# Last sequence of a fused Hawk and RWKV layer: gate chunks paired across the two gate weights, recurrences placed under gate products

## The chip, the cores and the metric

The kernel runs on one core of one Trainium2 chip. The metric is device time in microseconds. Three runs of the kernel before the change gave 657.23, 657.51 and 657.99 us, a median of 657.51 us.

## The reference

The input x has 8 sequences of 1024 tokens with 256 features, all in float32. The layer normalizes x, feeds the result to two blocks, and adds both to x:

```python
xn = _layernorm(x)
# block 1 (Hawk), 384 channels
gate = xn @ Wg.T ; u = xn @ Wi.T
y  = causal_depthwise_conv(u, conv_w, 4 taps) + conv_b
ig = sigmoid(y @ lru_Wi.T + lru_bi)
rg = sigmoid(y @ lru_Wg.T + lru_bg)
alpha = exp(-8 * softplus(lam) * rg)
beta  = sqrt(1 - alpha**2 + 1e-6)
h[t]  = alpha[t] * h[t-1] + beta[t] * ig[t] * y[t]     # along the tokens
hawk  = (gelu(gate) * h) @ Wo.T
# block 2 (RWKV channel mix), 256 channels
r = sigmoid(mix_r(xn) @ W_r.T) ; k = mix_k(xn) @ W_k.T
ffn = r * (square(relu(k)) @ W_v.T)
out = x + hawk + ffn
```

The recurrence over h is the only step that runs along the tokens. The product with Wo for a group of tokens needs gelu(gate) * h of all 384 channels for those tokens.

## The kernel before

**Layout.** Channels lie on the 128 partitions, tokens along the free dimension. The 384 channels are three chunks of 128 (HC = 3), numbered m = 0, 1, 2. A sequence of 1024 tokens has two halves of 512, L and R (HALVES). Tiles that matter here: y (the convolved input), tr (first tanh of the rg gate, then alpha), ti (tanh of the ig gate, then the input of the recurrence), q (first 1 - alpha**2, then beta, then h) and g (gelu(gate), then gelu(gate) * h). A sigmoid is computed as a tanh of half the argument, so ti has to be turned into (1 + ti) * 0.5 * beta * y before the recurrence.

**Gate products.** Both gate weights stand side by side in one tile w_l: rows 0 to 2 are the three chunks of the rg gate (they go to tr), rows 3 to 5 those of the ig gate (to ti). A Group (L194) makes two rows for both token halves at once. It uses a scheme with seven products in place of eight for two of the three input chunks, and adds the third input chunk with four plain products: 11 matmuls of 128x512 in all. The scheme needs sums of weight blocks (weight_sums, L157, on GpSimd, once per kernel for each family) and sums of token blocks (y_sums, L422, on GpSimd). Its five steps are s1 (2 matmuls), s2 (3), s3 (3), s4 (2) and s5 (1). Between them ScalarE copies a partial product to another bank and one to SBUF (seed L219, five L224), and VectorE adds them (fork_c L233, fork_d L247). After steps 2 to 5 ScalarE takes out one half of one row each through tanh (l_out, L326 and L329): row A half L after s2, row A half R after s3, row B half L after s4, row B half R after s5. In the kernel before, a group pairs rows 2*pair and 2*pair + 1: group 0 makes tr of chunks 0 and 1, group 1 makes tr of chunk 2 and ti of chunk 0, group 2 makes ti of chunks 1 and 2.

**Output products.** outs(s, t) (L597) makes the Wo product for two tiles of 128 tokens: six matmuls of 128x256 (by_token, L461, three chunks for each tile), then add_hawk (L505) adds the bank to the residual on VectorE and SyncE stores it. values (L591) does the same for the W_v product. A float32 matmul of the program is two MATMUL instructions in the profile.

**Recurrence.** For each chunk: decay (L538, Exp on ScalarE), decay_square (L542, Square on ScalarE), decay_rest (L545, VectorE), beta (L548, Sqrt on ScalarE), the input of the recurrence on VectorE, recur (L565, a scan on VectorE), and gated_state (L570, VectorE), which multiplies g by h. In sequences 0 to 6 the tail of this chain runs under the first products of the following sequence (chain, L606). The last sequence has no following one. There, all of the chain stands in the branch at L788 to L828, and the only PE work that is kept back for it is outs(s - 1, ...), the output products of the sequence before; the last four outs(s, ...) depend on the chain itself.

**Order.** Nothing is chosen by a scheduler. Every step is put into a list with a time (at, L183; pe, L186, which advances a clock by the length of a PE step), the list is sorted by that time (L836), and the instructions are issued in that order. The times are only sort keys: they fix the order on each engine's queue, and each engine then runs its queue in order, waiting for the semaphores of what it needs. There are eight PSUM banks, taken from and given back to a free list in the same order.

The branch before the change keeps d = now() right after the third step of group 1, and hangs the chain on it:

```python
for m in range(HC):
    at(d + [-2, -1.9, 0.2][m], decay, m)
    at(d + [-1, -0.9, 1][m], decay_square, m)
    at(d + [0, 1.2, 3][m], decay_rest, m)
    at(d + 3.1 + m / 10, beta, m)
    at(d + 9.2 + m / 10, weighted_input, m)
```

Of the kernel before, what the change touches and what calls it, by code (L numbers as in the profile page):

```python
# [32 lines left out]
def kernel(  # L33
# [120 lines left out]
    def block(family, row, c):  # L154
        return families[family][:, c, row * P : (row + 1) * P]

    def weight_sums(family):  # L157

        pairs = families[family].rearrange("p c (n r m) -> p c r n m", r=2, m=P)
        s = sums[family]  # L160
        a11, a12, a21, a22 = (pairs[:, c, r, :, :] for r in range(2) for c in range(2))
        nc.gpsimd.tensor_tensor(s[:, 0], a21, a22, ALU.add)
        nc.gpsimd.tensor_tensor(s[:, 1], s[:, 0], a11, ALU.subtract)
        nc.gpsimd.tensor_tensor(s[:, 2], a11, a21, ALU.subtract)
        nc.gpsimd.tensor_tensor(s[:, 3], a12, s[:, 1], ALU.subtract)
# [28 lines left out]
    class Group:  # L194


        def __init__(self, name, family, pair, chunk, tsum, out, third=None):
            self.name, self.family, self.pair, self.chunk, self.tsum = name, family, pair, chunk, tsum
            self.out, self.third = out, third
            self.bank = {}  # L200

        def step(self, n):
# [3 lines left out]
            def A(r, c):  # L206
                return block(self.family, 2 * self.pair + r, c)

# [116 lines left out]

    def l_out(gi, r, h, src):  # L326
        m = (2 * gi + r) % HC
        dst, b = (tr, HC) if 2 * gi + r < HC else (ti, 0)
        nc.scalar.activation(  # L329
            dst[:, m, HALVES[h]], src, AF.Tanh, bias=half_b[:, b + m : b + m + 1], scale=0.5  # L330
        )

    def u_group(s, gi):
# [3 lines left out]
            "u",  # L337
            gi,
            lambda c, h: xnT[:, c, 1 + h * NT : 1 + (h + 1) * NT],
            xsum,  # L340
            lambda r, h, src: place(gi, r, h, src),
        )

    def l_group(s, gi):
        return Group(
            f"l{gi}_{s}",
            "l",
            gi,
            lambda c, h: y[:, c, HALVES[h]],
            ysum,  # L350
            lambda r, h, src: l_out(gi, r, h, src),
            third=lambda h: y[:, 2, HALVES[h]],
        )
# [106 lines left out]

    def by_token(w, lhs, t, chunks):  # L461

        b = take()
        for j in range(2):
            for c in range(chunks):
                nc.tensor.matmul(  # L466
                    banks[b][:, j * D : (j + 1) * D],
                    lhs[:, c, (t + j) * P : (t + j + 1) * P],
                    weights[w][:, c, :],
                    start=(j == 0 and c == 0),  # L470
                    stop=True,
                    skip_group_check=True,
                )
        return b
# [27 lines left out]
    def o_product(s, t):  # L502
        token_bank["o", s, t] = by_token("o", gs[s % 2], t, HC)

# [52 lines left out]

    def weighted_input(m):

        nc.vector.scalar_tensor_tensor(q[:, m, :], q[:, m, :], 0.5, y[:, m, :], ALU.mult, ALU.mult)  # L560

    def opened_input(m, p):
        nc.vector.scalar_tensor_tensor(ti[:, m, p], ti[:, m, p], 1.0, q[:, m, p], ALU.add, ALU.mult)  # L563

    def recur(m, p=slice(0, S)):  # L565
# [24 lines left out]

    def values(s, t):  # L591
        pe(f"v{t}_{s}", 2, v_product, s, t)
        at(now() + 0.1, value, t)
        if t % 4 == 2:
            at(now() + 0.6, add_value, s, t // 4)

# [34 lines left out]
    with tc.manual_schedule():  # L631
# [61 lines left out]
        for s in range(B):  # L693
# [94 lines left out]
            else:  # L788
                gates(s, 4)
                gates(s, 6)  # L790
                values(s, 0)
                values(s, 2)
                at(now() - 1, y_sums)
                ls[0].step(1)
                values(s, 4)
                ls[0].step(2)
                ls[1].step(1)
                values(s, 6)
                ls[0].step(3)
                ls[1].step(2)  # L800
                ls[0].step(4)
                ls[2].step(1)
                ls[0].step(5)
                ls[1].step(3)
                d = now()
                outs(s - 1, 0)
                ls[1].step(4)
                ls[1].step(5)
                ls[2].step(2)
                outs(s - 1, 2, add=d + 13.6)  # L810
                ls[2].step(3)
                outs(s - 1, 4, add=d + 18)
                ls[2].step(4)
                ls[2].step(5)
                outs(s - 1, 6, add=d + 21.8)
                for t in range(0, TT, 2):
                    outs(s, t, 2)
                L, R = HALVES
                for m in range(HC):
                    at(d + [-2, -1.9, 0.2][m], decay, m)  # L820
                    at(d + [-1, -0.9, 1][m], decay_square, m)
                    at(d + [0, 1.2, 3][m], decay_rest, m)
                    at(d + 3.1 + m / 10, beta, m)
                    at(d + 9.2 + m / 10, weighted_input, m)
                for m, p, t in ((0, L, 13.2), (0, R, 13.3), (1, L, 13.5), (2, L, 20.3), (1, R, 20.4), (2, R, 21.3)):
                    for n, f in enumerate((opened_input, recur)):
                        at(d + t + 0.01 * n, f, m, p)
                    at(d + t + 0.03, gated_state, s, m, p)  # L828

# [66 lines left out]
```

## Time and profile before

| What | Value |
|---|---|
| Median of three runs | 657.51 us (657.23 to 657.99) |
| The profiled execution's own time | 657.73 us |
| Its span, first to last instruction | 655.9 us |
| PE busy | 646.9 us, 99% of the span |
| VectorE busy | 470.7 us, 72% |
| ScalarE busy | 430.3 us, 66% |
| GpSimd busy | 113.0 us, 17% |
| Mean granted TensorE clock | 0.995 |

The profile is of one execution. In the prediction its lines are in microseconds from the start of the span. In a timeline, the columns are the start, the time from the start of the first to the end of the last instruction of the group, the engine, the line of the kernel, the operation, output<-input, the number of instructions, and in brackets the idle time of the engine before the group with the work that ended it. Matmuls overlap, so the duration of a group is a little longer than the distance to the start of the next. PEclk is the share of full TensorE speed that the chip granted.

### The profile page before, as it was taken

The page shows a single profiled execution, that of the slowest core. Times are in us where ns is not written, and L with a number is a line of the kernel's source. Part 1 is how long each engine was busy: PE and PEld are TensorE (multiplying, and loading weights), DVE is VectorE, ACT ScalarE, POOL GpSimd, SP SyncE. Part 2 cuts the span into 40 slices and gives each one's busy share as a digit, 9 for nine tenths or more (in the row PEclk, how much of TensorE's full clock was granted, in tenths as well). Part 3 has the DMA queues.
Part 4 walks back from the last instruction along what each step waited for, and adds up shares of the span by engine and source line. Part 5 has one row for each costly group of instructions (what it writes and reads, how often), then busy time and mean ns, then how long its engine had stood idle before and what let it go on. Part 6 is the DMA issues. An engine that isn't in the chain of part 4 may idle for free.

```text
span 655.9 us, 5889 instructions
## 1 busy us (share of the span) xinstructions
PE 646.9 (99%) x2048; PEld 377.2 (58%) x2048; DVE 470.7 (72%) x604; ACT 430.3 (66%) x615; POOL 113.0 (17%) x82
## 2 busy tenths in 40 slices
PE   9999999999999999999999999999999999999987
PEld 4465446854477544775448654586445864466556
DVE  4778869755896659947599475993669844798295
ACT  4786877368782788727885388845878358772840
POOL 3606100430004300123003220042000430022000
PEclk9999999999999999999999999999999999999998
DMA  9402100031001400014000140001200011000012
GB/s 319 130 1 73 56 0 1 32 112 50 0 1 48 145 0 1 1 48 145 0 0 1 62 132 0 0 1 49 80 0 1 23 42 64 0 1 0 0 49 80
DMA packets 27550, 28.71 MB, mean 44 GB/s; under 512 B 1152, under 2 KB 27008, under 8 KB 27520
## 3 DMA queue, kind: packets, MB, share of 16 engines
q1 hardware_dynamic: 27104, 27.92, 12.9%
q10 hardware_dynamic: 416, 0.41, 0.2%
q8 instruction: 16, 0.26, 0.2%
q14 instruction: 14, 0.11, 0.1%
HBM read 19.94 MB, written 8.39 MB: 43 GB/s over the span
## 4 chain that ended last, share of the span: by engine, by line
PE 93%; DVE 4%; ACT 2%; issue 0%; DVEq 0%
PE bank L175 62%; PE bank L466 28%; PE bank L394 2%; PE bank L656 1%; DVE q L568 1%; ACT tr L540 1%; DVE q L560 1%; ACT q L543 0%; DVE g L572 0%; DVE ti L563 0%; DVE y L529 0%; DVE xr L439 0%; DVE res L510 0%; DVE st L367 0%; ACT L549 0%; ACT L540 0%
## 5 line engine op out<-in xcount | busy, mean ns | idle before, releaser
L175 PE MATMUL bank<-y,w_l 128*128 128x512 f32 x288 | 137.8, 592 | 0.0
L529 DVE SCALAR_TENSOR_TENSOR y<-u,par,y 128x1024 f32<-128x1024 f32 x72 | 94.3, 1326 | 1.2
L466 PE MATMUL bank<-w_o,g 128*128 128x256 f32 x384 | 89.9, 388 | 3.2 <-DVE g L572 3.1
L175 PEld LDWEIGHTS bank<-y,w_l 128*128 128x128 f32 x288 | 54.6, 190 | 62.6 <-issue 60.5
L466 PEld LDWEIGHTS bank<-w_o,g 128*128 128x128 f32 x384 | 74.8, 195 | 21.5 <-issue 6.2
L169 POOL TENSOR_TENSOR ysum<-y 128x512 f32<-128x512 f32 x8 | 16.9, 2106 | 385.4 <-PE bank L466 341.3
L175 PE MATMUL bank<-ysum,sum_l 128*128 128x512 f32 x144 | 72.4, 592 | 0.0
L219 ACT COPY bank<-bank 128x512 f32<-128x512 f32 x47 | 27.0, 575 | 66.2 <-PE bank L175 65.1
L233 DVE TENSOR_TENSOR bank<-bank,five 128x512 f32<-128x512 f32 x47 | 32.8, 698 | 51.4 <-PE bank L175 37.8
L175 PE MATMUL bank<-xsum,sum_u 128*128 128x512 f32 x138 | 69.1, 592 | 0.0
L329 ACT ACTIVATE tr<-bank,half_b 128x512 f32<-128x512 f32 x48 | 32.8, 684 | 54.5 <-PE bank L175 54.5
L175 PE MATMUL bank<-xk,w_k 128*128 128x512 f32 x128 | 60.1, 592 | 0.0
L466 PE MATMUL bank<-w_r,xr 128*128 128x256 f32 x256 | 57.7, 379 | 0.0
L466 PEld LDWEIGHTS bank<-w_r,xr 128*128 128x128 f32 x256 | 48.6, 190 | 13.1 <-issue 7.0
L175 PE MATMUL bank<-xnT,w_u 128*128 128x512 f32 x108 | 54.1, 593 | 0.2 <-ACT xnT L413 0.2
L466 PE MATMUL bank<-w_v,ysum 128*128 128x256 f32 x224 | 49.5, 379 | 0.0
L510 DVE TENSOR_TENSOR res<-res,bank 128x512 f32<-128x512 f32 (+1 forms) x36 | 22.0, 624 | 35.9 <-PE bank L466 35.9
L466 PEld LDWEIGHTS bank<-w_v,ysum 128*128 128x128 f32 x224 | 42.6, 190 | 5.8
L175 PEld LDWEIGHTS bank<-xsum,sum_u 128*128 128x128 f32 x138 | 26.1, 189 | 33.1 <-issue 31.2
L175 PEld LDWEIGHTS bank<-ysum,sum_l 128*128 128x128 f32 x144 | 26.8, 190 | 30.2 <-issue 28.5
L247 DVE TENSOR_TENSOR bank<-bank,five 128x512 f32<-128x512 f32 x24 | 16.7, 696 | 37.6 <-PE bank L175 37.6
L329 ACT ACTIVATE ti<-bank,half_b 128x512 f32<-128x512 f32 x48 | 30.3, 681 | 19.4 <-PE bank L175 19.3
(101 smaller groups left out, 1014.9 us busy)
## 6 DMA issues: line engine op xcount, KB each, us to landing
res<-in_x_dram SPq DMA_DIRECT2D x8, 1024.0 KB, 5.6
x<-in_x_dram SPq DMA_DIRECT2D x7, 1024.0 KB, 5.6
out_dram<-res SPq DMA_DIRECT2D x28, 256.0 KB, 2.1
x<-in_x_dram SPq DMA_DIRECT2D x4, 256.0 KB, 4.4
out_dram<-res SPq DMA_DIRECT2D x8, 128.0 KB, 1.8
w_l<-in_lru_wg_dram SPq DMA_DIRECT2D x1, 576.0 KB, 5.9
w_l<-in_lru_wi_dram SPq DMA_DIRECT2D x1, 576.0 KB, 6.9
w_u<-in_w_i_dram ACTq DMA_DIRECT2D x1, 384.0 KB, 4.0
```

Source lines behind the costliest of these rows:

```text
L169: nc.gpsimd.tensor_tensor(dst[:, 0, :], b12, b11, ALU.subtract)
L175: nc.tensor.matmul(banks[b], lhsT, rhs, start=start, stop=True, skip_group_check=True)
L219: nc.scalar.copy(banks[bank["B"]], banks[bank["A"]])
L233: nc.vector.tensor_tensor(banks[bank["C"]], banks[bank["B"]], self.five, ALU.add)
L247: nc.vector.tensor_tensor(d, banks[bank["B"]], self.five, ALU.add)
L329: nc.scalar.activation(dst[:, m, HALVES[h]], src, AF.Tanh, bias=half_b[:, b + m : b + m + 1], scale=0.5)
L394: nc.tensor.matmul(banks[b][:, t * P : (t + 1) * P], xs[s % 2][:, 4 * h + t, c * P : (c + 1) * P], ident, is_transpose=True, start=(t == 0 ...
L466: nc.tensor.matmul(banks[b][:, j * D : (j + 1) * D], lhs[:, c, (t + j) * P : (t + j + 1) * P], weights[w][:, c, :], start=(j == 0 and c == 0),
L510: nc.vector.tensor_tensor(o, o, two_tiles(b)[:, j : j + n, :], ALU.add)
L529: nc.vector.scalar_tensor_tensor(y[:, m, :], u[:, m, k : k + S], column(COL_CONV_W + k * HC + m), y[:, m, :], ALU.mult, ALU.add,)
L540: nc.scalar.activation(tr[:, m, :], tr[:, m, :], AF.Exp, bias=r, scale=r)
L560: nc.vector.scalar_tensor_tensor(q[:, m, :], q[:, m, :], 0.5, y[:, m, :], ALU.mult, ALU.mult)
```

## The change

Only the last sequence and its helpers change.

- Group gets its two rows as an argument. In the last sequence rows_of pairs row pair with row pair + 3: group 0 makes tr and ti of chunk 0, group 1 those of chunk 1, group 2 those of chunk 2. weight_sums is called a second time, for w_l with this pairing.
- The order of the PE steps of the last sequence is changed. Three of the four output products of the sequence before, outs(s - 1, 2), (4) and (6), stand behind the last gate product; outs(s - 1, 0) stands between the second and third step of group 2. d now marks the end of group 0, e the end of group 2.
- Two steps of VectorE for each chunk and half (weighted_input for the chunk, opened_input for the half) are replaced by gated_input and scaled_input, the pair that the earlier sequences use. The chains of chunks 0 and 1 are put under the products of groups 1 and 2, the scan of chunk 1 as one of 1024 tokens. Chunk 2 still goes in halves.
- In the first output product of the last sequence, the six matmuls go chunk by chunk (abreast) rather than token tile by token tile.
- The additions of the values (add_value) of the first half and of the output products of the sequence before stand at other places of VectorE's queue.

The diff:

```diff
@@ -154,9 +154,14 @@
     def block(family, row, c):
         return families[family][:, c, row * P : (row + 1) * P]
 
-    def weight_sums(family):
-
-        pairs = families[family].rearrange("p c (n r m) -> p c r n m", r=2, m=P)
+
+    def rows_of(pair, apart):
+        return (pair, pair + HC) if apart else (2 * pair, 2 * pair + 1)
+
+    def weight_sums(family, apart=False):
+
+        order = "p c (r n m) -> p c r n m" if apart else "p c (n r m) -> p c r n m"
+        pairs = families[family].rearrange(order, r=2, m=P)
         s = sums[family]
         a11, a12, a21, a22 = (pairs[:, c, r, :, :] for r in range(2) for c in range(2))
         nc.gpsimd.tensor_tensor(s[:, 0], a21, a22, ALU.add)
@@ -194,7 +199,8 @@
     class Group:
 
 
-        def __init__(self, name, family, pair, chunk, tsum, out, third=None):
+        def __init__(self, name, family, pair, rows, chunk, tsum, out, third=None):
+            self.rows = rows
             self.name, self.family, self.pair, self.chunk, self.tsum = name, family, pair, chunk, tsum
             self.out, self.third = out, third
             self.bank = {}
@@ -204,7 +210,7 @@
             S = [sums[self.family][:, i, self.pair, :] for i in range(4)]
 
             def A(r, c):
-                return block(self.family, 2 * self.pair + r, c)
+                return block(self.family, self.rows[r], c)
 
             bank = self.bank
             extra = 1 if third else 0
@@ -323,9 +329,9 @@
 
         return place
 
-    def l_out(gi, r, h, src):
-        m = (2 * gi + r) % HC
-        dst, b = (tr, HC) if 2 * gi + r < HC else (ti, 0)
+    def l_out(row, h, src):
+        m = row % HC
+        dst, b = (tr, HC) if row < HC else (ti, 0)
         nc.scalar.activation(
             dst[:, m, HALVES[h]], src, AF.Tanh, bias=half_b[:, b + m : b + m + 1], scale=0.5
         )
@@ -336,19 +342,22 @@
             f"u{gi}_{s}",
             "u",
             gi,
+            rows_of(gi, False),
             lambda c, h: xnT[:, c, 1 + h * NT : 1 + (h + 1) * NT],
             xsum,
             lambda r, h, src: place(gi, r, h, src),
         )
 
     def l_group(s, gi):
+        rows = rows_of(gi, s == B - 1)
         return Group(
             f"l{gi}_{s}",
             "l",
             gi,
+            rows,
             lambda c, h: y[:, c, HALVES[h]],
             ysum,
-            lambda r, h, src: l_out(gi, r, h, src),
+            lambda r, h, src: l_out(rows[r], h, src),
             third=lambda h: y[:, 2, HALVES[h]],
         )
 
@@ -458,19 +467,21 @@
         ka = key_home(s)
         nc.scalar.activation(ka[:, :, HALVES[h]], ka[:, :, HALVES[h]], AF.Square)
 
-    def by_token(w, lhs, t, chunks):
+    def by_token(w, lhs, t, chunks, abreast=False):
 
         b = take()
-        for j in range(2):
-            for c in range(chunks):
-                nc.tensor.matmul(
-                    banks[b][:, j * D : (j + 1) * D],
-                    lhs[:, c, (t + j) * P : (t + j + 1) * P],
-                    weights[w][:, c, :],
-                    start=(j == 0 and c == 0),
-                    stop=True,
-                    skip_group_check=True,
-                )
+        order = [(j, c) for j in range(2) for c in range(chunks)]
+        if abreast:
+            order.sort(key=lambda jc: jc[1])
+        for j, c in order:
+            nc.tensor.matmul(
+                banks[b][:, j * D : (j + 1) * D],
+                lhs[:, c, (t + j) * P : (t + j + 1) * P],
+                weights[w][:, c, :],
+                start=(j == 0 and c == 0),
+                stop=True,
+                skip_group_check=True,
+            )
         return b
 
     token_bank = {}
@@ -500,7 +511,7 @@
         nc.vector.scalar_tensor_tensor(o, tf[:, 4 * h : 4 * h + 4, :], 0.5, o, ALU.mult, ALU.add)
 
     def o_product(s, t):
-        token_bank["o", s, t] = by_token("o", gs[s % 2], t, HC)
+        token_bank["o", s, t] = by_token("o", gs[s % 2], t, HC, s == B - 1 and t == 0)
 
     def add_hawk(s, t, pieces=1):
         b = token_bank.pop(("o", s, t))
@@ -555,13 +566,6 @@
     def scaled_input(m, p=slice(0, S)):
         nc.vector.scalar_tensor_tensor(ti[:, m, p], ti[:, m, p], 0.5, q[:, m, p], ALU.mult, ALU.mult)
 
-    def weighted_input(m):
-
-        nc.vector.scalar_tensor_tensor(q[:, m, :], q[:, m, :], 0.5, y[:, m, :], ALU.mult, ALU.mult)
-
-    def opened_input(m, p):
-        nc.vector.scalar_tensor_tensor(ti[:, m, p], ti[:, m, p], 1.0, q[:, m, p], ALU.add, ALU.mult)
-
     def recur(m, p=slice(0, S)):
 
         before = 0.0 if p.start == 0 else q[:, m, p.start - 1 : p.start]
@@ -588,11 +592,11 @@
         pe(f"r{t}_{s}", 2, r_product, t)
         at(now() + 0.1, r_tanh, t)
 
-    def values(s, t):
+    def values(s, t, add=0.6):
         pe(f"v{t}_{s}", 2, v_product, s, t)
         at(now() + 0.1, value, t)
         if t % 4 == 2:
-            at(now() + 0.6, add_value, s, t // 4)
+            at(now() + add, add_value, s, t // 4)
 
     def outs(s, t, pieces=1, add=0):
         pe(f"o{t}_{s}", 3, o_product, s, t)
@@ -789,43 +793,64 @@
                 gates(s, 4)
                 gates(s, 6)
                 values(s, 0)
-                values(s, 2)
+                values(s, 2, 8)
+                at(b + 8, weight_sums, "l", True)
                 at(now() - 1, y_sums)
                 ls[0].step(1)
                 values(s, 4)
                 ls[0].step(2)
                 ls[1].step(1)
+                ls[0].step(3)
                 values(s, 6)
-                ls[0].step(3)
+                ls[0].step(4)
                 ls[1].step(2)
-                ls[0].step(4)
+                ls[0].step(5)
+                d = now()
                 ls[2].step(1)
-                ls[0].step(5)
                 ls[1].step(3)
-                d = now()
-                outs(s - 1, 0)
                 ls[1].step(4)
                 ls[1].step(5)
                 ls[2].step(2)
-                outs(s - 1, 2, add=d + 13.6)
+                outs(s - 1, 0, add=d + 15.2)
                 ls[2].step(3)
-                outs(s - 1, 4, add=d + 18)
                 ls[2].step(4)
                 ls[2].step(5)
-                outs(s - 1, 6, add=d + 21.8)
+                e = now()
+                outs(s - 1, 2, add=e + 6)
+                outs(s - 1, 4, add=e + 7)
+                outs(s - 1, 6, add=e + 8)
                 for t in range(0, TT, 2):
                     outs(s, t, 2)
                 L, R = HALVES
-                for m in range(HC):
-                    at(d + [-2, -1.9, 0.2][m], decay, m)
-                    at(d + [-1, -0.9, 1][m], decay_square, m)
-                    at(d + [0, 1.2, 3][m], decay_rest, m)
-                    at(d + 3.1 + m / 10, beta, m)
-                    at(d + 9.2 + m / 10, weighted_input, m)
-                for m, p, t in ((0, L, 13.2), (0, R, 13.3), (1, L, 13.5), (2, L, 20.3), (1, R, 20.4), (2, R, 21.3)):
-                    for n, f in enumerate((opened_input, recur)):
-                        at(d + t + 0.01 * n, f, m, p)
-                    at(d + t + 0.03, gated_state, s, m, p)
+                at(d - 4, decay, 0)
+                at(d - 3, decay_square, 0)
+                at(d - 2, decay_rest, 0)
+                at(d + 5.2, decay, 1)
+                at(d + 5.3, decay_square, 1)
+                at(d + 6.5, decay_rest, 1)
+                at(d + 10.2, beta, 0)
+                at(d + 10.3, beta, 1)
+                at(d + 17.2, decay, 2)
+                at(d + 17.3, decay_square, 2)
+                at(e - 1.5, decay_rest, 2)
+                at(e + 0.2, beta, 2)
+                at(d + 1.2, gated_input, 0)
+                at(d + 11.3, scaled_input, 0)
+                at(d + 15.16, recur, 0, L)
+                at(d + 15.17, recur, 0, R)
+                at(e + 0.4, gated_state, s, 0, L)
+                at(e + 0.5, gated_state, s, 1, L)
+                at(e + 2.0, gated_state, s, 0, R)
+                at(e + 2.1, gated_state, s, 1, R)
+                at(d + 9, gated_input, 1)
+                at(d + 15.4, scaled_input, 1)
+                at(d + 15.5, recur, 1)
+                at(e - 0.5, gated_input, 2, L)
+                at(e + 1.7, gated_input, 2, R)
+                for p, t in ((L, 1.4), (R, 4.4)):
+                    at(e + t, scaled_input, 2, p)
+                    at(e + t + 0.1, recur, 2, p)
+                    at(e + t + 0.2, gated_state, s, 2, p)
 
         def constants():
             nonlocal rate
```

## The prediction, written before the changed kernel was run

> **What bounds the kernel now.** I first read the busy shares and the 40 slices of the page, then TensorE's waits, then the last 30 us of its timeline. The page shows PE busy all the way, with one dip in the last two slices:
>
> ```profile
> span 655.9 us, 5889 instructions
> PE 646.9 (99%) x2048; PEld 377.2 (58%) x2048; DVE 470.7 (72%) x604; ACT 430.3 (66%) x615; POOL 113.0 (17%) x82
> PE   9999999999999999999999999999999999999987
> PEclk9999999999999999999999999999999999999998
> ```
>
> PE bounds the kernel, so only PE's idle time, a slow PE clock, and what lies after the last matmul can be won. PE's waits for the whole span (engine line <- releaser: us in total, times, longest) and the end of its timeline say where that is:
>
> ```profile
> PE bank L466 <- DVE g L572: 3.1, 1, 3.1
> PE bank L656 <- DVE five L632: 1.2, 1, 1.2
> PE bank L175 <- DVE g L247: 0.9, 1, 0.9
> ...
> 631.00 1.88 PE L175 MATMUL bank<-y,w_l 128*128 128x512 f32 x4
> 632.72 4.00 PE L466 MATMUL bank<-w_o,g 128*128 128x256 f32 x16
> 639.79 12.62 PE L466 MATMUL bank<-w_o,g 128*128 128x256 f32 x44 [3.08 <-DVE g L572]
> ```
>
> After the last gate product PE has outs(s - 1, 6) (12 instructions) and two thirds of a tile of the last sequence (4), and then waits for gated_state of chunk 2, half L. The 44 instructions after that take 12.62 us, 0.287 us each, while 12 such take 2.60 us in the middle of the stage (614.64 to 617.24), 0.217 us each. The table by stretches says why (columns: stretch and length; busy us of PE, PEld, DVE, ACT, POOL; PEclk; DMA):
>
> ```profile
> 636.20:639.80 3.60, 0.52 (x3) 0.12 (x2) 3.53 (x6) 0.00 (x0) 0.00 (x0) 0.86 0.43 146
> 639.80:643.00 3.20, 3.20 (x8) 2.57 (x9) 3.12 (x4) 0.00 (x0) 0.00 (x0) 0.50 0.00 0
> 643.00:646.00 3.00, 3.00 (x10) 2.41 (x9) 2.94 (x5) 0.00 (x0) 0.00 (x0) 0.56 0.00 0
> 646.00:652.40 6.40, 6.40 (x30) 5.31 (x28) 1.79 (x5) 0.00 (x0) 0.00 (x0) 1.00 0.49 164
> ```
>
> The gap halves the granted clock until about 645.6. Fed without a gap at full clock, the 60 instructions from 632.72 would take 60 x 0.2165 = 13.0 us and start their last at about 645.5, ending near 645.9; they end at 652.41. So 6.5 us are to be won: 3.6 us of gap (632.72 + 16 x 0.2165 = 636.19, resumed 639.79) and 2.9 us of half clock. No more: the tail from 652.41 to 655.9 (3.5 us of two additions, an issue and a store) stays.
>
> VectorE and ScalarE in the gap show why g is late. VectorE runs the chain without a break, and begins it only when Sqrt ends, behind two table loads:
>
> ```profile
> 621.49 1.28 ACT L549 ACT_TABLE_LOAD   x1
> 622.79 3.23 ACT L549 ACTIVATE q<-q,beta_eps 128x1024 f32<-128x1024 f32 x3
> ...
> 623.97 3.50 DVE L560 SCALAR_TENSOR_TENSOR q<-q,y 128x1024 f32<-128x1024 f32 x3 [0.56 <-ACT q L549]
> 627.38 0.69 DVE L247 TENSOR_TENSOR bank<-bank,five 128x512 f32<-128x512 f32 x1
> 628.05 0.69 DVE L563 SCALAR_TENSOR_TENSOR ti<-ti,q 128x512 f32<-128x512 f32 x1
> 628.77 1.23 DVE L568 TENSOR_TENSOR_SCAN q<-tr,ti 128x512 f32<-128x512 f32 x1
> ```
>
> **The change, part by part.** PE's own work is unchanged: 33 gate matmuls at 0.858 us start to start (599.18 to 600.04 and its like), two W_v products at 1.73 us, eight output products at 2.60 us from 593.17 on, 28.3 + 3.5 + 20.8 = 52.6 us, so 645.7. In the new order, if nothing waits: group 0 ends at 610.3; group 1 s3 to s5 ends at 617.2; s2 of group 2 619.8, outs(s - 1, 0) 622.4, s3 624.9, s4 626.7, s5 627.5; the three kept products end at 635.3; then the last four.
>
> *More weight sums on POOL*: four 128x384 additions; the earlier four took 0.99, 0.99, 1.01 and 2.04 us. POOL stands idle 44.1 us before y_sums at 583.3, and the last reader of the old sums starts at 553.62, so 5 us fit. They share time with VectorE: the convolution steps there (L529) take 1.28 us at the median and 2.17 us beside POOL. Two or three of VectorE's steps may be 0.9 us longer between 547 and 556; fork_c at 550.46 serves a matmul at 553.62, and fork_d at 554.84 one at 557.06. Free; without that cover, 1 to 2 us.
>
> *Gate steps and forks.* Group 0 s3 now follows group 1 s1, without the W_v product between: its second matmul (601.76) needs fork_c, whose product starts at 598.33 and is readable 1.08 us later (matmul 593.17, copy 594.28), so it is done at 600.1. add_value stands behind it now and before fork_d, which ends at 602.7 and is needed at 605.2. Group 1's forks end at 610.4 and 613.8, needed at 612.9 and 614.6. Nothing waits.
>
> *ScalarE*: three table loads become four (Exp, Sqrt, back to tanh and Exp, Sqrt). From its queue: Exp and Square of chunk 0 end at 608.9, of chunk 1 at 617.9; tanh of chunk 2 L ends at 619.9, load 621.2, beta 0 622.4, beta 1 623.5, load 624.8, tanh of chunk 2 R 625.8 (its product is ready at 625.1), Exp 627.1, Square 628.2, two tanhs 629.5, load 630.8. Here a rule speaks against the change: the Trainium skill, "ScalarE: Activation LUTs", section "What ACT_TABLE_LOAD costs", gives each switch of set a drain of about 1.38 us beside a load of 1.28. The row says otherwise: load at 621.49, Sqrt at 622.79, so 1.30 us in all. By the page, beta 0 is 1.4 us late, fork_d of group 2 ends at 625.7 where PE wants it at 624.9, and beta 2 ends at 635.7; the two stalls sum to about 1.5 us. By the row there is none. I take the row.
>
> *VectorE* decides. Start to start: 0.61 us for a 128x512 step, 1.16 for a 128x1024 one, 0.72 where the next needs it, 1.26 to 1.32 for a half scan. A 1024 scan is in no row: not under one half (1.22), not over two (2.50); I take 2.50, as a longer step saves little. From beta 0: scaled_input 0 at 622.4; fork_d of group 2 623.6 to 624.3 (needed 624.9); scans of chunk 0 at 624.2 and 625.5; add_hawk 626.7; scaled_input 1 627.3; scan 1 628.5; decay_rest 2 631.0 to 631.7, so beta 2 ends at 632.9; meanwhile gated_input 2 L 631.6, gated_state 0 L and 1 L 632.2 and 632.8; scaled_input 2 L 633.4, scan 634.1, gated_state 2 L 635.4 to 636.1; gated_input 2 R 636.0, gated_state 0 R and 1 R 636.6 and 637.2, scaled_input 2 R 637.8, scan 638.5, gated_state 2 R 639.8 to 640.5.
>
> PE wants chunks 0 and 1 L at 635.3 and 636.2 and chunk 2 L, thanks to the order by chunks, at 637.1 (without it at 636.2, about when it is there); half R at 640.5 to 641.4. The margins are 1.0 us on L and 0.9 on R. The tightest before is fork_d of group 2, 0.6 us. The banks of the last products were all emptied by 628.9.
>
> *The end.* The three additions of outs(s - 1, ...) now come at 640.4 to 642.3, so three 256 KB stores and eight of 128 KB, 1.8 MB, leave after 641. The stretch from 8 to 16 us moved 368 GB/s, so 1.8 MB needs 5.0 us of transfer from about 642, and the last store is issued at 646.6 anyway. Hidden; if queued, 0 to 0.5 us.
>
> Sum: 645.9 + 3.5 = 649.4 us of span, 6.5 less. The profiled execution took 657.73 us, 1.83 over its span, and stands 0.22 over the median: 649.4 + 1.83 - 0.22 = 651.0 us.
>
> **The rivals.** *Small stalls remain.* The VectorE chain is 18 us without slack; table loads by the page, or steps 5 to 10% longer, put PE 0.5 to 3 us behind: 651.8 to 654.0 us. Against it: durations come from the same shapes in the same stage.
>
> *A second half clock.* The clock fell within the gap, about 2.6 us after PE fell quiet (0.86 over 3.6 us is 1.0 us at half). A gap of that length before the last products again brings 2.9 us of half clock: 651.0 + 2.6 + 2.9, about 656.5 us. The page "TensorE: Matmul & The Clock Gate", section "What's actually happening", lets the clock back after about 3.4 us of work, which would price the half clock at 1.7 us and the whole gain at 5.3; this trace kept it 5.8 us, so I use 2.9. The gap must come from chunk 2 being 3.6 us later than worked out.
>
> *Slower than before.* Same place, chunk 2 L: everything of it stands behind chunk 1's 1024 scan and three table loads. The gap and its half clock outweigh 6.5 + 1.3 us only if gated_state 2 L is 5.9 us late, at 642; that takes about 3.7 us for each table switch, where rows show 1.30. About 660 us there.
>
> *The change does nothing*: only if PE still waited 3 us for the same g. The chain of chunks 0 and 1 is off the end by the built order of the queues, so this falls under the second rival.
>
> **How the numbers follow.** PE fed: 0.74, 650.4 to 651.8. Small stalls: 0.15. Second half clock: 0.06. Slower: 0.05, with causes I don't see. 651.0 is the first case; the range of 8 in 10 reaches into the second, 650.3 to 653.4. Differences under 0.2% (1.3 us) are about what a measurement cannot tell from none. Faster 0.93, same 0.02, slower 0.05.
>
> **What would show it.** Right: PE's wait for g gone or under 0.5 us, PEclk 1.00 in the last 12 us, the last eight output products 2.60 us apart, ScalarE loads of 1.28 followed at once by work, scan 1 at or under 2.5 us. Wrong: a wait of PE for g of chunk 2 or for fork_d of group 2, a PEclk of 0.50 near the end, the tail after the last matmul over 4 us, or longer VectorE steps beside POOL before 560.

## The result and the profile after

The changed kernel takes 652.11 us (median of four runs, 651.00 to 652.19) against 657.37 us before (657.15 to 657.99): a ratio of 0.9915, 95% interval 0.9897 to 0.9932. That is 5.3 us less. The forecast was 651.0 us, range 650.3 to 653.4. The profiled execution took 652.18 us with a span of 650.4 us.

The page of the changed kernel, the same lines as shown of before:

```profile
span 650.4 us, 5894 instructions
PE 644.3 (99%) x2048; PEld 375.5 (58%) x2048; DVE 471.2 (72%) x602; ACT 431.9 (66%) x616; POOL 117.5 (18%) x86
PEclk9999999999999999999999999999999999999999
```

The dip of the clock in the last slice is gone. All that PE waited for in the whole execution (columns as before):

```profile
PE bank L660 <- DVE five L636: 1.2, 1, 1.2
PE bank L180 <- DVE g L253: 0.9, 1, 0.9
PE bank L403 <- DVE x L396: 0.3, 1, 0.3
PE bank L180 <- ACT xnT L422: 0.2, 1, 0.2
```

The 3.1 us for g of the recurrence (gated_state, L572 before, L576 now) are not there any more, and no other wait in the last sequence has come in their place. The 0.9 us for g is for another step, fork_d (L247 before, L253 now); it stands in the profile of before with the same 0.9 us. The 0.3 us for x is new; it lies in the first 15 us of the program, which the change does not touch, and it comes back below. PE's timeline, first gate product of the last sequence and the end:

```profile
594.22 1.02 PE L180 MATMUL bank<-y,w_l 128*128 128x512 f32 x2
...
628.59 18.29 PE L477 MATMUL bank<-w_o,g 128*128 128x256 f32 x84
```

84 instructions, the three kept products (36) and the four last ones (48), run in one piece at 0.217 us each. The table by stretches (columns as before: PEclk is third from the right):

```profile
640.00:642.00 2.00, 2.00 (x11) 1.74 (x11) 1.97 (x4) 0.00 (x0) 0.00 (x0) 1.00 0.00 0
642.00:644.00 2.00, 2.00 (x11) 1.77 (x10) 2.00 (x6) 0.00 (x0) 0.00 (x0) 1.00 0.69 231
644.00:646.00 2.00, 2.00 (x11) 1.77 (x10) 0.97 (x3) 0.00 (x0) 0.00 (x0) 1.00 1.00 343
```

The clock stays at 1.00. The delayed stores fill the DMA engines (share 1.00, 343 GB/s), but PE works on beside them.

The last sequence's first gate product starts at 594.22 us, 1.05 us later than in the profile of before (593.17). So the fair measure of the change is from that product to the end of the span. I call it the stage:

| Kernel | Stage starts | Span ends | Stage |
|---|---|---|---|
| before | 593.17 | 655.9 | 62.73 |
| changed | 594.22 | 650.4 | 56.18 |

The stage is 6.55 us shorter; the forecast said 6.5. Both profiles are of one execution each. The medians fell by 5.3 us, 1.2 less than that, and why is taken up in the section on the prediction.

### The profile page after: what moved, and what is told of

Read it like the earlier page. It is cut to its first block, busy times and chain, and to the rows that moved or that the text cites. A ratio compares the mean times of both kernels' runs of the same rounds, so it can differ in the third digit from the quotient of the medians.

```text
span 650.4 us, 5894 instructions
## 1 busy us (share of the span) xinstructions
PE 644.3 (99%) x2048; PEld 375.5 (58%) x2048; DVE 471.2 (72%) x602; ACT 431.9 (66%) x616; POOL 117.5 (18%) x86
## 4 chain that ended last, share of the span: by engine, by line
PE 97%; DVE 2%; ACT 0%; issue 0%; DVEq 0%
PE bank L180 64%; PE bank L477 30%; PE bank L403 2%; PE bank L660 1%; DVE y L540 0%; DVE xr L448 0%; DVE st L376 0%; DVE g L253 0%; ACT x L398 0%; DVE half_b L678 0%; DVE bank L239 0%; DVE xnT L420 0%; ACT xnT L422 0%; ACT u L323 0%; DVE mv L378 0%
## 5 line engine op out<-in xcount | busy, mean ns | idle before, releaser
L477 PE MATMUL bank<-w_o,g 128*128 128x256 f32 x384 | 86.1, 379 | 0.0
L477 PEld LDWEIGHTS bank<-w_o,g 128*128 128x128 f32 x384 | 73.0, 190 | 15.9 <-issue 5.3
L239 DVE TENSOR_TENSOR bank<-bank,five 128x512 f32<-128x512 f32 x47 | 32.8, 698 | 49.1 <-PE bank L180 35.4
L180 PEld LDWEIGHTS bank<-xk,w_k 128*128 128x128 f32 x128 | 24.3, 190 | 30.7 <-issue 30.4
```

The source lines that it names most:

```text
L180: nc.tensor.matmul(banks[b], lhsT, rhs, start=start, stop=True, skip_group_check=True)
L239: nc.vector.tensor_tensor(banks[bank["C"]], banks[bank["B"]], self.five, ALU.add)
L477: nc.tensor.matmul(banks[b][:, j * D : (j + 1) * D], lhs[:, c, (t + j) * P : (t + j + 1) * P], weights[w][:, c, :], start=(j == 0 and c == 0),
```

## The experiments

My theory: the gain is the gap before the last products plus the half clock that the gap sets off, and it needs both parts of the change, the chunk-wise pairing that lets two of three recurrences run under the gates and the 7.8 us of kept products behind the last gate. The main rivals: the slow instructions after the gap have another cause than the clock; moving products alone does it; pairing and early recurrences alone do it. Each run below gives one profile, and its stage is worked out as above.

**The gap filled, nothing else changed.**

```diff
 outs(s - 1, 6, add=d + 21.8)
+at(now(), fill, 4)   # take a bank, four times matmul(bank, ident, y[:, 0, 0:NT]), give it back
```

> The kernel before, with four extra 128x512 float32 matmuls (0.86 us each, 3.4 us, into a bank nobody reads) put between the last kept product and the first output product of the last sequence, so that TensorE works through the gap. Nothing else changes, and VectorE delivers chunk 2 half L at the same moment. Theory (gap and half clock are two costs, 3.6 and 2.9 us): the granted clock stays at 1.00, the last 44 instructions take 0.217 us each, TensorE ends near 649.5 in place of 652.4, and the time falls by 2.9 us to about 654.5. Rival (the slow instructions after the gap are slow because half R of g is late, not because of the clock): the extra matmuls change nothing, about 657.4 us, with a wait for g in their place.

655.90 us (median of six) against 657.68 us for the kernel before, measured with it, ratio 0.9972, interval 0.9959 to 0.9984. PE's end of this kernel:

```profile
636.25 3.60 PE L682 MATMUL bank<-y,ident 128*128 128x512 f32 x8
639.68 10.94 PE L466 MATMUL bank<-w_o,g 128*128 128x256 f32 x48
```

and its clock there:

```profile
640.00:642.00 2.00, 1.97 (x10) 1.41 (x9) 1.97 (x3) 0.00 (x0) 0.00 (x0) 1.00 0.00 1
642.00:644.00 2.00, 2.00 (x11) 1.77 (x10) 1.93 (x4) 0.00 (x0) 0.00 (x0) 1.00 0.00 0
644.00:646.00 2.00, 2.00 (x11) 1.57 (x9) 1.97 (x3) 0.00 (x0) 0.00 (x0) 1.00 0.00 0
```

In the same stretch where the kernel before shows a clock of 0.50, this one shows 1.00, although VectorE delivers g no sooner: half L of chunk 2 is through 46.57 us after the stage's start in both. The stage is 654.1 - 594.11 = 59.99 us, 2.74 less than before. So the half clock is a cost by itself, about as sized (2.9); the rival falls. The median moved by 1.8 us and not by 2.9. I don't know how much of the rest is the start (this profile's stage starts 0.94 us later) and how much the half clock of the other executions of before: their mean granted clock lies between 0.995 and 0.997, so 0.3 to 0.5% of 656 us, 2.0 to 3.3 us, is lost clock (a part of it falls into the gap itself, where it costs nothing). The profile of before is one at 0.995. The length of the half clock is taken up again below.

**Only the output products moved behind the gates.** All four of them move here, also outs(s - 1, 0), which the change leaves between the steps of group 2.

```diff
-outs(s - 1, 0) ... outs(s - 1, 2, add=d + 13.6) ... outs(s - 1, 4, add=d + 18) ... outs(s - 1, 6, add=d + 21.8)
# at each of the four old places the clock of the sort keys still advances by 3
+for t in range(0, TT, 2):          # behind ls[2].step(5)
+    at(now(), o_product, s - 1, t)
+    at(d + 21.8 + t / 100, add_hawk, s - 1, t)
```

> The kernel before, with only the four output products of the sequence before moved behind the last gate product, old pairing, old chain. Rival (work behind the gates is all that was missing): 651 to 652 us, no wait for g. Theory (the chain starts only after the one Sqrt for all three chunks, so moving products takes their cover from the forks of group 2): TensorE waits for fork_c of group 2 about 2.2 us and for fork_d about 3.6 us, because both stand in VectorE's queue behind decay_rest and weighted_input; 655 us if the clock stays up, up to 659 us if the second stall halves it.

658.34 us (one run). Its waits of PE:

```profile
PE bank L175 <- DVE bank L233: 2.9, 1, 2.9
PE bank L175 <- DVE bank L247: 0.7, 1, 0.7
```

and their places in its timeline:

```profile
624.21 1.60 PE L175 MATMUL bank<-ysum,sum_l 128*128 128x512 f32 x2 [2.90 <-DVE bank L233]
...
629.47 1.12 PE L175 MATMUL bank<-ysum,w_l 128*128 128x512 f32 x2 [0.73 <-DVE bank L247]
```

No wait for g of the recurrence is left, and yet little is won: the stage is 656.6 - 594.51 = 62.09 us, 0.64 less than before. The products had covered fork_c and fork_d of group 2 (L233, L247). In VectorE's queue fork_c stands behind decay_rest of all three chunks, and fork_d behind weighted_input of all three, which waits for Sqrt. The first wait was 2.9 us where 2.2 were expected, the second 0.7 where 3.6 were. The clock fell to 0.50 at 624.7, half a microsecond after PE had resumed, and the six instructions between the two waits took 4.5 us in place of 2.6, so that fork_d was nearly there when PE came to it. Moving all the products is not enough: the rival falls in this form. A milder one, with outs(s - 1, 0) left in front of the fork and the old chain kept, was not run.

**The changed kernel without its cover behind the gates.**

```diff
 ls[1].step(5)
+at(now(), o_product, s - 1, 2); at(now(), o_product, s - 1, 4)
 ls[2].step(2)
 outs(s - 1, 0, add=d + 15.2)
 ls[2].step(3)
+at(now(), o_product, s - 1, 6)
 ls[2].step(4); ls[2].step(5); e = now()
-outs(s - 1, 2, add=e + 6); outs(s - 1, 4, add=e + 7); outs(s - 1, 6, add=e + 8)
+# the three add_hawk at the same keys as before this edit
```

> The changed kernel, with its three kept output products taken from behind the gates and put back among them: two between groups 1 and 2, one between the third and fourth step of group 2. Pairing, chain and queue orders of ScalarE and VectorE stay. Theory: the gates of group 2 come 5.2 us later, so do beta of chunk 0 and all that follows on VectorE; gated_state of chunk 2 L ends about 5.2 us later, with 1.4 us of margin in the changed kernel, so TensorE stands about 3.8 us before the third chunk of the first output product, and the half clock after it adds up to 2.9: 656 to 659 us. Rival (pairing and early recurrences alone suffice): 652 us, no gap.

658.99 us (one run); the stage is 657.2 - 594.37 = 62.83 us, 6.65 more than in the changed kernel and as long as in the kernel before. Its wait for g:

```profile
PE bank L477 <- DVE g L576: 3.4, 2, 2.3
```

the end of its timeline:

```profile
638.95 2.52 PE L477 MATMUL bank<-w_o,g 128*128 128x256 f32 x8 [2.28 <-DVE g L576]
642.62 11.07 PE L477 MATMUL bank<-w_o,g 128*128 128x256 f32 x40 [1.16 <-DVE g L576]
```

and its clock:

```profile
640.00:642.00 2.00, 1.46 (x5) 0.63 (x3) 1.93 (x3) 0.00 (x0) 0.00 (x0) 0.55 0.00 0
642.00:644.00 2.00, 1.38 (x3) 1.18 (x4) 2.00 (x4) 0.00 (x0) 0.00 (x0) 0.50 0.00 0
```

The sum came as expected (656 to 659 us), the place only in part: of the two waits the first, 2.3 us, is for chunk 0 (PE resumes at 638.95 when gated_state 0 L is through, which stands behind the scan of chunk 1 on VectorE), and only 1.2 us are for chunk 2. With the new pairing and the new chain the cover behind the gates is still needed: without it the whole gain is gone. The pairing alone, with the old chain, was not tried: the old order of ScalarE and VectorE asks for gates that come later with the new pairs. Nor were the parts of the new chain (the other pair of VectorE steps, the single scan for chunk 1, the moved additions) taken apart.

**The first output product tile by tile.**

```diff
-token_bank["o", s, t] = by_token("o", gs[s % 2], t, HC, s == B - 1 and t == 0)
+token_bank["o", s, t] = by_token("o", gs[s % 2], t, HC)
```

> The changed kernel without the chunk by chunk order in the first output product of the last sequence. Theory: chunk 2 L is wanted 0.87 us earlier, and it is there 1.4 us before the present need, so nothing changes: within 0.3 us of the changed kernel, apart from the spread at the start of the run. Rival (the order by chunks is needed): a wait for g of up to 0.9 us.

651.20 us (one run), stage 649.4 - 593.25 = 56.15 us, no wait for g. The order by chunks does nothing at present; it is a reserve of 0.87 us.

**How far the chain is from the path.** Extra additions on VectorE, four or eight, into a tile nobody reads:

```diff
+at(e + 1.35, idle_steps, 4)        # or 8
 for p, t in ((L, 1.4), (R, 4.4)):
```

> The changed kernel with four extra 128x512 additions (0.61 us each, 2.44 us, into a tile nobody reads) on VectorE ahead of scaled_input of chunk 2 L. Theory (chunk 2 has 1.4 us of margin and nothing else is near): TensorE waits about 1.0 us for g at the third chunk of the first output product, at most 0.1 more at half R, the clock stays at 1.00, 1.1 us over the changed kernel from the first gate product on. Rival (VectorE is nowhere near the path): no wait at all.

> The same with eight extra additions, 4.9 us. Theory: a gap of about 3.4 us, the clock halves as in the kernel before, so 3.5 us of waits plus 2 to 3 us of half clock: 5.5 to 6.5 us over the changed kernel, most of the gain gone. If the clock holds: 3.5 us over it.

654.37 and 657.27 us (one run each). PE's end with four:

```profile
628.84 9.66 PE L477 MATMUL bank<-w_o,g 128*128 128x256 f32 x44
639.75 9.04 PE L477 MATMUL bank<-w_o,g 128*128 128x256 f32 x40 [1.25 <-DVE g L576]
```

and with eight, with its clock after the gap below:

```profile
627.56 9.66 PE L477 MATMUL bank<-w_o,g 128*128 128x256 f32 x44
641.38 10.59 PE L477 MATMUL bank<-w_o,g 128*128 128x256 f32 x40 [4.16 <-DVE g L576]
```

```profile
642.00:644.00 2.00, 2.00 (x8) 1.66 (x7) 1.96 (x4) 0.00 (x0) 0.00 (x0) 0.65 0.00 0
644.00:646.00 2.00, 2.00 (x7) 1.55 (x6) 1.97 (x3) 0.00 (x0) 0.00 (x0) 0.50 0.00 0
```

An addition took 0.70 us and not 0.61 (2.78 us for four, 5.69 for eight, from the first addition to the start of the next step). With four, PE resumes at 639.75 where it would have gone on at 628.84 + 44 x 0.2165 = 638.37: 1.38 us late, so the margin is 2.78 - 1.38 = 1.4 us, as read from the profile after. With eight, the same sum gives 641.38 - 637.09 = 4.29 us and again 1.4. The stages are 58.13 and 62.30 us, 1.95 and 6.12 over the changed kernel. The first is 0.85 more than I expected: 0.3 from the dearer additions, 0.2 within the last 40 instructions (9.04 us in place of 8.83), and 0.3 in a tail of 3.8 us: SyncE, which issues the delayed stores first, ends its last issue 0.8 us after the last addition, and 0.5 us after it in the changed kernel. After the 1.4 us gap the clock stays at 1.00; after the 4.3 us gap it falls, and the 40 instructions take 1.8 us longer. (The idle time in brackets is a little less than these gaps, since it is counted from the end of the last matmul.)

**The start of the run.** In the changed kernel the stage began 1.05 us late. I ran it again, then with fewer warm-up matmuls:

```diff
-busy(26)
+busy(22)
```

> The changed kernel again, unchanged, on the chip and in the rounds of the other runs here. About 651 to 652.2 us. Theory: from the first gate product of the last sequence to the last matmul it takes 52.6 us as in the first profile, and what differs between its executions is the start: the end of the 26 warm-up matmuls between 8.1 and 9.6 us.

> The changed kernel with 22 in place of 26 warm-up matmuls at the start of the program (0.22 us each at full clock, 0.43 at half). Theory (what put the profiled execution 1.05 us behind is that its 26 warm-ups ended at 8.8 us in place of 8.1, and the transposes wait behind them although their data are there at 8.4): the first transposes start at about 8.4 us, and the median falls by 0.4 to 0.8 us against the changed kernel. Rival (the start is set by loads and by the normalization): no difference.

The changed kernel again: 652.05 us (651.17 to 652.35, five runs), ratio to before 0.9917, interval 0.9903 to 0.9931; the stage of its profile is 649.4 - 593.21 = 56.19 us. With 22 warm-ups: 651.35 us (651.20 to 652.04, four runs), ratio 0.9910, interval 0.9896 to 0.9923. The intervals overlap. Its stage is 649.6 - 593.41 = 56.19 us, and there are executions near 652 in both, so the number of warm-ups is at most a part of it. The profiles show a second step. PE's first 15 us in the changed kernel as first profiled:

```profile
1.19 7.77 PE L660 MATMUL bank<-five 128*128 128x512 bf16 x26 [1.19 <-DVE five L636]
8.80 1.04 PE L403 MATMUL bank<-ident,x 128*128 128x128 f32 x8
...
14.43 1.44 PE L403 MATMUL bank<-ident,x 128*128 128x128 f32 x8 [0.30 <-DVE x L396]
```

The transposes come at 8.80 (8.13 before), and the second ones wait for x, 1.06 us later than before. VectorE and GpSimd of the same profile there:

```profile
9.87 0.69 DVE L420 COPY xnT<-bank 128x512 f32<-128x512 f32 x1 [1.85 <-PE bank L403]
10.48 0.91 DVE L678 TENSOR_SCALAR half_b<-par 128x6 f32<-128x6 f32 x1
```

```profile
10.36 1.00 POOL L169 TENSOR_TENSOR sum_u<-w_u 128x384 f32<-128x384 f32 x1
```

half_b, six columns wide, takes 0.91 us and ends at 11.39, 0.03 us after the GpSimd step here. In the profile of before it starts at 9.88 and ends at 10.33, 0.03 us after the GpSimd step before that one (9.31 to 10.30). A start that is 0.6 us late becomes one that is 1.0 us late, because the small step has to sit out one GpSimd step more; and behind it stand the statistics and the normalization that the second transposes wait for. So I moved the two small steps as well:

```diff
-busy(26)
+busy(22)
-at(0.02, parameters)
+at(0.07, parameters)
```

> The changed kernel with 22 warm-up matmuls and with the two small parameter steps of VectorE (half_b and mu_rest, 0.4 to 0.9 us beside GpSimd's weight sums) moved from before the statistics of the second token half to behind its normalization. Theory (the last sequence starts late, near 594.2 in place of 593.2, when the second transposes at 13.4 to 14.4 us wait for that normalization, which stands behind these steps): in all executions the last sequence starts at 593.2 or earlier, 650.9 to 651.4 us, no execution at 652 or above. Rival (the late start comes from loads): the same two clusters near 651.2 and 652.1 us.

650.75 us (650.62 to 650.92, four runs) against 657.71 us, ratio 0.9894, interval 0.9878 to 0.9911. half_b takes 0.17 us in its new place, the second transposes start without a wait, and the stage starts at 592.74 us. No execution is near 652. The late start does not belong to the change: the two runs made from the kernel before (gap filled, products moved) start their stage at 594.11 and 594.51. With the parameter steps moved as well, all eight executions of this run and the next lie between 650.16 and 650.93 us. The warm-ups' own part stays: in the next run, with the same start, the first transposes come at 8.91 us in place of 7.82 and the stage starts at 593.47.

**A shorter tail.** On top of it, the last output product in two single tiles:

```diff
-for t in range(0, TT, 2):
+for t in range(0, TT - 2, 2):
     outs(s, t, 2)
+for t in range(TT - 2, TT):         # three matmuls, one addition, one store for each
+    pe(f"o{t}_{s}", 1.5, o_single, s, t)
+    at(now() + 0.1, add_single, s, t)
```

> The same with the last output product split into its two token tiles, each with a bank, an addition and a store of its own. Theory (behind the last matmul stand two additions one after the other, the second 0.33 us behind the first, and then the store): the tail falls from 3.5 to about 3.1 us, 0.3 to 0.4 us less than the run before this one, 650.5 to 651.0 us. Rival (the tail is set by the queue of stores): no difference.

650.35 us (650.16 to 650.93, four runs) against 657.71 us, ratio 0.9889, interval 0.9875 to 0.9904. Its end:

```profile
643.38 2.75 PE L529 MATMUL bank<-w_o,g 128*128 128x256 f32 x12
...
646.17 0.42 DVE L541 TENSOR_TENSOR res<-res,bank 128x256 f32<-128x256 f32 x1 [0.87 <-PE bank L529]
```

From the last matmul (646.13) to the end of the span (649.1) it takes 3.0 us in place of 3.5, and the stage is 55.63 us. In the medians it is 0.4 us ahead of the run before it, with ranges that overlap, so the profile shows this gain and the times only allow it. It is the fastest version here, 1.1% under the kernel before.

## Why the prediction was right

**The bound and what was to be won.** The stage got 6.55 us shorter, where the sum said 6.5. The filled gap measured the half clock alone at 2.74 us in its profile, and undoing the cover brought back 6.65 us. The 6.5 us is what the profiled execution of before could win, though, and not every execution. In the profiles the half clock lasts either 3.41 or 6.83 us (see the last section): 6.83 in the profile of before, whose mean clock is 0.995. Of the 25 executions of before whose clock is on record, 7 show 0.995, 5 show 0.996 and 13 show 0.997, which is what 3.41 us at half would give (3.41 x 0.5 / 656 = 0.3%). By my estimate such an execution loses 1.7 us in place of 2.9 and has 3.6 + 1.7 = 5.3 us to win. These are the two figures, 1.7 and 5.3, that the prediction had worked out and set aside. That the medians fell by just 5.3 us proves nothing by itself, since the start of the run moves them too; no execution of before at 0.997 was profiled.

**PE's own work.** The last matmul was put at 645.9 in the time of the profile before, which is 646.95 with the 1.05 us of later start; it ended at 646.88.

**GpSimd's second weight sums.** They ran from 546.3 to 557.3, waiting for the old sums' readers. Two decay_rest steps beside them took 0.98 and 1.19 us in place of 0.69; the prediction had expected it of the convolution steps. It had named longer VectorE steps here as a sign of being wrong. The sign appeared, but PE shows no wait.

**ScalarE.** Here the page "ScalarE: Activation LUTs" of the Trainium skill (section "What ACT_TABLE_LOAD costs") had spoken against the change, and the row was taken. ScalarE of the changed kernel:

```profile
620.89 1.28 ACT L560 ACT_TABLE_LOAD   x1
622.19 2.19 ACT L560 ACTIVATE q<-q,beta_eps 128x1024 f32<-128x1024 f32 x2
624.39 1.28 ACT L335 ACT_TABLE_LOAD   x1
626.21 0.69 ACT L335 ACTIVATE tr<-bank,half_b 128x512 f32<-128x512 f32 x1 [0.54 <-PE bank L180]
```

The first switch costs 1.30 us from load to work; there is no drain of 1.38 us to be seen behind it. The 0.54 us of idle time after the second load is a wait for the gate product, and behind the third, at 630.43, ScalarE waits 0.58 us for decay_rest of chunk 2.

**VectorE.** The end of the chain in the changed kernel:

```profile
623.37 1.22 DVE L567 SCALAR_TENSOR_TENSOR ti<-ti,q 128x1024 f32<-128x1024 f32 x1 [1.40 <-ACT q L560]
...
629.39 2.29 DVE L572 TENSOR_TENSOR_SCAN q<-tr,ti 128x1024 f32<-128x1024 f32 x1
...
635.97 0.69 DVE L576 TENSOR_TENSOR g<-g,q 128x512 f32<-128x512 f32 x1
...
640.42 0.69 DVE L576 TENSOR_TENSOR g<-g,q 128x512 f32<-128x512 f32 x1
```

With 1.05 us added, scaled_input 0 was put at 623.45 and came at 623.37; gated_state 2 L was to end at 637.15 and ended at 636.66; 2 R at 641.55 and ended at 641.11. The largest single part of the difference, 0.2 us, is the 1024 scan, 2.29 us in place of 2.50. So the margins are 1.4 us on L and 1.3 on R (the third chunk of R is wanted at 642.45) and not 1.0 and 0.9. fork_d of group 2, the tightest step ahead of them, ended at 625.20, 0.8 us before PE came to it (626.01); 0.6 had been worked out.

**The end.** The tail from the last matmul is 3.5 us, as before; the stores of the kept products stayed hidden, as sized.

**What was off.** The median is 1.1 us above the forecast. The term is the last line of the sum, 649.4 + 1.83 - 0.22: it took the start of the profile before as the start of every execution. The stage starts between 593.2 and 594.5 us over the eight profiles with 26 warm-ups after the first, and the two profiles of the changed kernel differ by 1.01 us there with stages of 56.18 and 56.19 us. Of this nothing was in the range by reason; it fell inside the width that was kept for small stalls, which did not happen. That the median lies inside the range is, to that extent, luck. In the third rival the "3.7 us for each table switch" has no working: 5.9 us over three loads would be 2.0 more each, 3.3 in all.

## What to carry to other kernels

A gap on TensorE near the end of a program should be priced with the slow clock after it, here 1.8 us where the half clock lasted 3.41 us and 2.7 to 2.9 where it lasted 6.83. Closing it took two things at once here: something that TensorE can do while the last dependent chain runs, and a chain short enough for that cover. In the forms tried, the first alone gave 0.6 us and the second alone nothing. Where changes are below 1%, time the stage from its own first instruction in the profile, since the start of the program can move by a microsecond.

## What the runs showed of the hardware that I had not expected

Read in steps of 0.1 us, the traces show when the clock fell and how long it stayed at half. Idle is PE's idle time before the matmul at which it resumed:

| Run | Idle | PE resumes | Clock falls | Clock back | At half |
|---|---|---|---|---|---|
| four additions | 1.25 | 639.75 | not before the end of the work | | |
| no cover behind the gates | 2.28 | 638.95 | 640.22 | 647.05 | 6.83 |
| products moved alone | 2.90 | 624.21 | 624.73 | 628.14 | 3.41 |
| before | 3.08 | 639.79 | 638.79 | 645.61 | 6.83 |
| eight additions | 4.16 | 641.38 | 642.61 | 646.02 | 3.41 |

```profile
640.20:640.30 0.10, 0.10 (x2) 0.10 (x1) 0.10 (x1) 0.00 (x0) 0.00 (x0) 0.59 0.00 0
647.00:647.10 0.10, 0.10 (x2) 0.05 (x1) 0.10 (x2) 0.00 (x0) 0.00 (x0) 0.77 0.00 0
...
642.60:642.70 0.10, 0.10 (x2) 0.10 (x1) 0.10 (x1) 0.00 (x0) 0.00 (x0) 0.53 0.00 0
646.00:646.10 0.10, 0.10 (x2) 0.10 (x1) 0.10 (x1) 0.00 (x0) 0.00 (x0) 0.91 0.00 0
```

(Columns as in the table by stretches. The first two lines are of the run without cover, the other two of the run with eight additions; a clock between 0.50 and 1.00 tells where in the 0.1 us it changed.) So the fall need not come within the gap: in three of the four runs it came 0.5 to 1.3 us after PE had resumed, in the run without cover even before its second wait. The half clock lasted 3.41 us or twice that. In the two runs with twice that, PE stood idle for 1.0 and 1.2 us within the first 3.41 us; in the other two it did not. That is four cases, and no run tested it.

The warm-ups run at two speeds. Their weight loads are 0.43 us apart up to 4.0 us in the profile of before, up to 5.3 in that of the changed kernel and up to 7.0 in that of the products moved alone, and closer to 0.22 afterwards, while the row of the granted clock says 1.00 throughout. The transposes behind them start at 8.13, 8.80 and 9.62 us.

VectorE's small parameter steps are held beside GpSimd's sums. In each of the ten profiles with these steps in their old place, one of the two (half_b in nine, mu_rest in the filled gap) ends 0.02 to 0.04 us after the GpSimd step that runs, after 0.34 to 1.00 us where 0.17 is enough. This agrees with the Trainium skill ("SBUF — State Buffer", section "SBUF: two separate sides"): the two engines share a port pair that one of them holds for a whole instruction. The page names VectorE operations with two SBUF inputs or in a two-port mode; half_b has one input, and the runs don't show its mode. The batch statistics that took their place in the queue were not slowed (0.74 us for two, in both places).

An addition of 128x512 into the same tile again and again took 0.70 us, where additions into different tiles start 0.61 us apart.
